# A two-layer graph network on 128 graphs: other step orders in the first two groups and the last, one statistic later in every cycle, other banks and store queues at the end

## The chip, the cores and the metric

The kernel runs on one core of one Trainium2 chip. The metric is the device time of one execution in microseconds (us); the median of several runs is compared. The engines are TensorE (PE in the profile, its weight loads PEld), VectorE (DVE), ScalarE (ACT), GpSimd (POOL) and SyncE (SP). Each works through its own queue of instructions in order.

## The reference

There are 128 graphs of 128 nodes with 512 features, all float32, and one adjacency matrix for all. Two layers follow each other; cut to what matters:

```python
# layer 0
h = relu(layernorm(x))
q, k, v = h @ Wq.T, h @ Wk.T, h @ Wv.T
rel = adj.T * (q @ k.T);  rel = rel / norm(rel, axis=2)
x = x + rel @ v
# layer 1, 8 heads of 64
h = relu(layernorm(x))
q, k, v = h @ Wq + bq, h @ Wk + bk, h @ Wv + bv
weights = softmax(q @ k.T / 8 + where(adj == 0, -1e9, 0))     # per head
x = x + weights @ v
```

## The kernel before

**Groups.** The graphs go through in 32 groups of 4 (b = 0 to 3). In a cycle three neighbouring groups are in work at once. The names in the lists of steps are: `p` the layer 1 that is being finished, `l` the layer 1 in work, `n` the layer 1 that begins, `m` the layer 0 in work, `f` the layer 0 that begins (its loads and statistics). The same object moves from `f` to `m` and from `n` to `l` to `p` (`run`, line 691, and the loop behind it).

**The order is written out by hand.** The scheduling is manual on all five engines (line 704). A step such as `l.wt0` is the method `wt(0)` of `l`; `l.Q.P1` is a step of its product Q. Each step issues instructions to several engines, and every engine executes its own in the order of the list. So a step that waits holds up everything that later steps put on the same engine. Four lists exist: FIRST (line 657, group 0), SECOND (664, group 1), ORDER (673, groups 2 to 31), LAST (684, what is left after the loop).

**Products.** A product (Q, K, V, or G, layer 0's combined query and key matrix) of a group's 512x512 block takes seven blocks of 8 matmuls, P1 to P7, in place of eight, with sums of quarters of weights and inputs formed ahead (`sumA`, `sumB`). It uses three PSUM banks x, y, z of the pool `ps_mm` (4 banks). P1 writes x and its result is kept as r1, P2 writes y and r1 is added on DVE, P5 writes z and is kept as r5, P6 adds to x and is kept as r2, P3 adds to z and r2 is added, P7 adds to x and r5 is added, P4 adds to x and is copied. P7 may only write x once r2 has been read from it, P4 only once P7's sum has been read. "Kept" is a copy on ACT, but on DVE for layer 1's V (line 246, with the bias).

**Layer 0.** `R` (line 393) multiplies, `mask_rel` (402, DVE) masks the result out of its PSUM bank, `square`, `N` and `norms` give the norms, `O` and `xO` (433, 439) the output, added to x. `O2` and `O3` read v's second half, which P4 copies on ACT.

**Layer 1.** `S` (471) makes a graph's scores for 8 heads: into one double bank `ps_s` (there is one), or, for b == 1, into the two banks of the pool `ps_o`, one half each. `mk`, or `add_mask` and `mx`, or `mkA` and `mkB` for halves, add the mask and take the maximum on DVE (483 to 488, 541 to 544); `ex`, or `exC`/`exD`, `exA`/`exB` for halves, take the exponential on ACT (495, 524, 554) and end with a DMA that sends the weights to DRAM in 32x32 blocks (`send_blocks`, line 195, on ACT's queue). `wr` fetches them back (203, SP's queue, 4 DMAs into the pool `tpool`, 2 buffers), and `wt` (508, 510) turns the blocks on DVE, so that the weights stand transposed. `A` (616) multiplies them with v, `oc` (627, ACT) copies and sends the outcome, `rdo` fetches it, and `ot` (639 to 652) turns it on DVE, scales it by 1/sum, adds x on POOL and stores to `out` on POOL's queue. The buffers of exponentials, sent inputs and outcomes are the tag "e" of the pool `npool` (3 slots). A slot is handed out in the order in which the slots were given up in the list.

In LAST the last two graphs go another way: `tw` (565, 566) transposes the weights on PE through PSUM banks of `ps_o`, ACT copies them, `An` (576) multiplies, and `fin` (585, 593, 594) scales on DVE, adds x and stores on SP's queue.

**The next input.** `hn` (312, ACT) normalizes two graphs and sends them, `rd` fetches, `T` (324, DVE) turns them. `stat` (294, 295, DVE) and `inv` (301 to 304, POOL) prepare its scale and shift.

Of the kernel before, what the change touches and what calls it, by code (L numbers as in the profile page):

```python
# [21 lines left out]
def kernel(  # L22
# [418 lines left out]
    class Layer1(Layer):  # L441
# [16 lines left out]
        def S(self, b):  # L458
            g = self.g

            if b == 1 and g < NG - 1:
                half = [ps_o.tile([P, NH, P], F32, tag="po", name=f"pso_{g}_{r}") for r in range(2)]
            else:
                pss = ps_s.tile([P, 2, NH, P], F32, tag="ps", name=f"pss_{g}_{b}")
                half = [pss[:, r] for r in range(2)]
                self.ps[b] = pss.rearrange("p r k j -> p (r k) j")
            self.half_s[b] = half
            for k in range(NH):
                for r in range(2):
                    rows = slice(r * HD, (r + 1) * HD)  # L470
                    nc.tensor.matmul(  # L471
                        half[r][:, k, :],
                        lhsT=self.qT[rows, k, ts(b, P)], rhs=self.kT[rows, k, ts(b, P)],
                        start=True, stop=True,
                    )
# [72 lines left out]
        def ex_r(self, b, r):  # L548
            g, sc, nmax = self.g, self.ps[b], self.nmax[b]
            if r == 0:  # L550
                self.total[b] = small.tile([P, H], F32, tag="total", bufs=4, name=f"total_{g}_{b}")
                self.e[b] = npool.tile([P, H, P], F32, tag="e", name=f"en_{g}_{b}")
            for i in range(r * NH, (r + 1) * NH):
                nc.scalar.activation(
                    self.e[b][:, i, :], sc[:, i, :], AF.Exp,
                    bias=nmax[:, i : i + 1], accum_out=self.total[b][:, i : i + 1],
                )
# [12 lines left out]
        def An(self, b):  # L570

            po, wT = ps_o.tile([P, D], F32, tag="po", name=f"pn1_{self.g}_{b}"), self.wT.pop(b)
            for r in range(2):
                for k in range(NH):
                    i = 2 * k + r
                    nc.tensor.matmul(
                        po[:, ts(i, HD)], lhsT=wT[:, r * NH + k, :], rhs=self.v[:, b, ts(i, HD)],
                        start=True, stop=True,
                    )
            self.po[b] = po  # L580

        def fin(self, b):
            g, xb = self.g, x_tiles.pop((self.g, b))
            o = work.tile([P, D], F32, tag="o", name=f"o_{g}_{b}")
            nc.vector.tensor_tensor(
                o.rearrange("p (k r d) -> p k r d", k=NH, r=2),
                self.po.pop(b).rearrange("p (k r d) -> p k r d", k=NH, r=2),
                self.rs.pop(b).rearrange("p (r k) -> p k r", r=2)[:, :, :, None].to_broadcast(
                    [P, NH, 2, HD]
                ),  # L590
                ALU.mult,
            )
# [37 lines left out]
        def rdo(self, i):  # L630
            self.uo[i] = fetch_blocks(self.do.pop(i), 2, f"o_{self.g}_{i}")

        def ot(self, i):
            g, u = self.g, self.uo.pop(i)
            for n in range(2):
                b = 2 * i + n
                xb = x_tiles.pop((g, b))
                o = work.tile([P, NH, TB, BK], F32, tag="o", name=f"o_{g}_{b}")
                nc.vector.transpose(
                    o.rearrange("p k t q -> p t k q"),  # L640
                    u[:, n * TB : (n + 1) * TB].rearrange("p t (k q) -> p t k q", q=BK),
                )
                heads = o.rearrange("p k t q -> p k (t q)").rearrange("p k (r d) -> p k r d", r=2)
                nc.vector.tensor_tensor(  # L644
                    heads, heads,
                    self.rs.pop(b).rearrange("p (r k) -> p k r", r=2)[:, :, :, None].to_broadcast(
                        [P, NH, 2, HD]
                    ),
                    ALU.mult,
                )  # L650
                nc.gpsimd.tensor_tensor(xb, xb, o.rearrange("p k t q -> p (k t q)"), ALU.add)  # L651
                nc.gpsimd.dma_start(out[g * G + b], xb)

# [102 lines left out]
```

## Time and profile before

| | |
|---|---|
| median of 3 runs | 2506.55 us (2505.88 to 2507.48) |
| profiled execution, whole | 2507.47 us |
| its span, first to last instruction | 2505.70 us |
| PE busy / DVE busy / ACT busy / POOL busy | 2488.6 / 1716.3 / 1024.3 / 531.5 us |
| granted TensorE clock, mean | 0.998 |
| one ordinary cycle (Q.P1 of one group to Q.P1 of the next) | 76.73 us |
| PE's last matmul ends at | 2497.43 us |

Times are microseconds from the span's start. In the views of groups and waits a line reads: line, engine, operation, output <- inputs, number, then busy time and mean, then idle time ahead. In a view of waits it reads: who waited for whom, total, times, longest. In a view of stretches it reads: the stretch, its length, the busy time of PE, PEld, DVE, ACT and POOL with the number of instructions, the granted clock (1.00 is full speed), the DMA engines' share and GB/s. Ends of matmuls are modelled, so starts are the surer times.

### The profile page before, as it was taken

To read this page: it belongs to the slowest core of one execution; us is meant where nothing else is said; L and a number is where in the kernel's file an instruction comes from. 1 tells how busy PE (TensorE), PEld (TensorE's weight loads), DVE (VectorE), ACT (ScalarE), POOL (GpSimd) and SP (SyncE) were. 2 spreads that over 40 slices of the span, in tenths; PEclk is the share of its full clock that TensorE was granted. 3 is DMA by queue.
4 is the path that set the end of the run, shared out by engine and by line. 5 is a ranking of instruction groups with operands and counts; after the bars stand their busy time and mean duration, and the time that the engine had idled before them with its cause. 6 is when DMAs were issued, how large, how long until landed. Compare 5 with 4: busy or idle time off the path is not lost.

```text
span 2505.7 us, 40908 instructions
## 1 busy us (share of the span) xinstructions
PE 2488.6 (99%) x14688; PEld 2114.5 (84%) x14688; DVE 1716.3 (68%) x2547; ACT 1024.3 (41%) x3248; POOL 531.5 (21%) x944
## 2 busy tenths in 40 slices
PE   9999999999999999999999999999999999999998
PEld 7788888888888888888888888888888888888887
DVE  6467766667766677666677666776667776667766
ACT  3334434344434444343434344443434443444433
POOL 5011212212221212122121211221221212112211
PEclk9999999999999999999999999999999999999999
DMA  6155644555544555455564455554455644455543
GB/s 207 60 169 168 189 142 156 162 177 177 161 153 153 178 164 190 139 159 169 168 185 156 155 152 179 166 184 145 151 169 169 193 147 153 155 177 177 166 137 118
DMA packets 370476, 405.72 MB, mean 162 GB/s; under 512 B 29601, under 2 KB 286753, under 8 KB 370273
## 3 DMA queue, kind: packets, MB, share of 16 engines
q1 hardware_dynamic: 279520, 168.97, 25.3%
q10 hardware_dynamic: 69856, 165.70, 17.6%
q0 software_dynamic: 20896, 68.44, 8.3%
q8 instruction: 116, 1.90, 0.3%
q14 instruction: 88, 0.71, 0.1%
HBM read 204.80 MB, written 198.18 MB: 161 GB/s over the span
## 4 chain that ended last, share of the span: by engine, by line
PE 95%; DMA 2%; DVE 1%; ACT 1%; issue 0%; SPq 0%; POOL 0%; ACTq 0%; DVEq 0%; POOLq 0%
PE pv_x L229 17%; PE pg_x L229 9%; PE pv_z L229 9%; PE pk_x L229 8%; PE pq_x L229 8%; PE pg_z L229 5%; PE pq_z L229 4%; PE po L616 4%; PE pr L393 4%; PE pk_z L229 4%; PE po L433 4%; PE pv_y L229 4%; PE pss L471 4%; PE pg_y L229 2%; PE pk_y L229 2%; PE pq_y L229 2%
## 5 line engine op out<-in xcount | busy, mean ns | idle before, releaser
L651 POOL TENSOR_TENSOR xb<-xb,o 128x512 f32<-128x512 f32 x124 | 158.0, 1274 | 1205.6 <-DVE o L644 1204.1
L229 PE MATMUL pv_x<-wc_v,h 128*128 128x256 f32 x1280 | 303.8, 384 | 0.0
L229 PEld LDWEIGHTS pv_x<-wc_v,h 128*128 128x128 f32 x1280 | 238.0, 190 | 58.6 <-issue 20.8
L229 PE MATMUL pv_z<-wc_v,s 128*128 128x256 f32 x1024 | 245.9, 383 | 0.0
L312 ACT ACTIVATE hn<-xb,shift,rstd 128x512 f32<-128x512 f32 x252 | 191.0, 807 | 127.0 <-POOL shift L304 124.8
L324 DVE STREAM_TRANSPOSE h<-u_h 128x1024 f32<-128x1024 f32 x126 | 156.1, 1239 | 107.1 <-DMA u_h<-d_h 106.9
L229 PEld LDWEIGHTS pv_z<-wc_v,s 128*128 128x128 f32 x1024 | 192.6, 190 | 28.9 <-issue 0.2
L495 ACT ACTIVATE e<-pss,nmax 128x128 f32<-128x128 f32 x512 | 179.9, 381 | 89.5 <-DVE nmax L488 75.0
L627 ACT COPY oT<-po 128x512 f32<-128x512 f32 x124 | 72.6, 586 | 274.1 <-PE po L616 274.1
L229 PE MATMUL pq_x<-h,wc_q 128*128 128x256 f32 x768 | 181.8, 380 | 0.9 <-DVE h L324 0.8
L229 PE MATMUL pv_x<-wc_v,s 128*128 128x256 f32 x768 | 181.7, 379 | 0.0
L229 PE MATMUL pk_x<-h,wc_k 128*128 128x256 f32 x768 | 181.5, 379 | 0.0
L294 DVE BATCH_NORM_STATS2 st<-xb 128x6 f32<-128x512 f32 x256 | 170.8, 667 | 8.4 <-DMA xb<-in_x_dram 8.4
L510 DVE STREAM_TRANSPOSE wT<-u_w 128x1024 f32<-128x1024 f32 x126 | 153.4, 1218 | 21.0 <-DMA u_w<-d_w 18.4
L229 PEld LDWEIGHTS pq_x<-h,wc_q 128*128 128x128 f32 x768 | 145.4, 190 | 22.1 <-PE pv_x L229 2.0
L229 PEld LDWEIGHTS pk_x<-h,wc_k 128*128 128x128 f32 x768 | 145.8, 190 | 19.9
L229 PEld LDWEIGHTS pv_x<-wc_v,s 128*128 128x128 f32 x768 | 143.3, 190 | 18.4 <-issue 0.2
L644 DVE TENSOR_TENSOR o<-o,rs 128x512 f32<-128x512 f32 x124 | 124.4, 1003 | 4.3
L229 PE MATMUL pg_z<-s,wc_a 128*128 128x256 f32 x512 | 124.1, 385 | 0.0
L301 POOL TENSOR_SCALAR rstd<-mv 128x2 f32<-128x2 f32 x128 | 28.4, 222 | 447.5 <-DVE mv L295 445.2
L616 PE MATMUL po<-wT,v 128*64 128x128 f32 x1984 | 122.0, 276 | 0.0
L229 PE MATMUL pq_z<-s,wc_q 128*128 128x256 f32 x512 | 121.6, 380 | 0.3
(157 smaller groups left out, 4834.5 us busy)
## 6 DMA issues: line engine op xcount, KB each, us to landing
d_h<-hn ACTq DMA_DIRECT2D x126, 512.0 KB, 3.6
u_h<-d_h SPq DMA_DIRECT2D x504, 128.0 KB, 3.5
d_w<-e ACTq DMA_DIRECT2D x126, 512.0 KB, 2.7
u_w<-d_w SPq DMA_DIRECT2D x504, 128.0 KB, 3.2
xb<-in_x_dram POOLq DMA_DIRECT2D x124, 256.0 KB, 3.1
d_o<-oT ACTq DMA_DIRECT2D x62, 512.0 KB, 3.0
u_o<-d_o SPq DMA_DIRECT2D x248, 128.0 KB, 2.9
out_dram<-xb POOLq DMA_DIRECT2D x124, 256.0 KB, 3.0
```

The lines of the kernel that those rows point to most:

```text
L229: nc.tensor.matmul(ps[:, m, :], lhsT=lhsT, rhs=rhs, start=first and m == 0 and k == 0, stop=k == 1, skip_group_check=True,)
L294: nc.vector.bn_stats(st, x_tiles[g, b])
L312: nc.scalar.activation(hn[:, r], x_tiles[g, b].rearrange("p (k j q) -> p j k q", j=TB, q=BK), AF.Relu, bias=self.shift[:, b : b + 1], scal ...
L324: nc.vector.transpose(half.rearrange("p k (t i) -> p t k i", i=BK), self.u.pop(i).rearrange("p t (k q) -> p t k q", q=BK),)
L393: nc.tensor.matmul(pr[:, b, :], lhsT=self.turned(k, b), rhs=self.gT[:, k, ts(b, P)], start=(k == 0), stop=(k == KD - 1),)
L433: nc.tensor.matmul(po, lhsT=self.rel[:, b, :], rhs=self.v[:, b, :], start=True, stop=True)
L471: nc.tensor.matmul(half[r][:, k, :], lhsT=self.qT[rows, k, ts(b, P)], rhs=self.kT[rows, k, ts(b, P)], start=True, stop=True,)
L495: nc.scalar.activation(e[:, :, i, :], sc[:, i, :].rearrange("p (j q) -> p j q", q=BK), AF.Exp, bias=nmax[:, i : i + 1], accum_out=self.tot ...
L510: nc.vector.transpose(self.wT[b].rearrange("p h (t i) -> p t h i", i=BK), self.uw.pop(b).rearrange("p t (h q) -> p t h q", q=BK),)
L616: nc.tensor.matmul(po[r * HD : (r + 1) * HD, k, :], lhsT=self.v[:, b, ts(2 * k + r, HD)], rhs=wT[:, r * NH + k, :], start=True, stop=True,)
L644: nc.vector.tensor_tensor(heads, heads, self.rs.pop(b).rearrange("p (r k) -> p k r", r=2)[:, :, :, None].to_broadcast([P, NH, 2, HD]), ALU ...
L651: nc.gpsimd.tensor_tensor(xb, xb, o.rearrange("p k t q -> p (k t q)"), ALU.add)
```

## The change

In FIRST, `f.G.P1` and `f.sumA` come before the last two outputs of layer 0, `n.T0` before `f.G.P7`, `n.Q.P1` before `f.G.P4`, and `w.sumk` later. In SECOND, `l.wt0` comes after `l.wr1`. In ORDER, `f.stat3 f.inv1` come after `l.V.P6`. In LAST, `p.A1 p.oc1 p.rdo1` come right after `l.S0`, graph 1 and graph 3 take their scores in halves from `ps_o`, `l.wt0` and the steps around it stand elsewhere, the last `ot` is split in two, the transposes `tw` use `ps_mm`, the last graph's `An` and `fin` are done in two halves, the sum with x of graph 2 moves from DVE to POOL, and the last stores go to SP's and ACT's queues. The last `rdo` fetches into a slot of tag "e".

```diff
-    def fetch_blocks(d, n: int, name: str):
+    def fetch_blocks(d, n: int, name: str, pool=tpool, tag="u"):
-        u = tpool.tile([P, n * TB, 8 * BK // n], F32, tag="u", name=f"u_{name}")
+        u = pool.tile([P, n * TB, 8 * BK // n], F32, tag=tag, name=f"u_{name}")
...
         def S(self, b):
-            if b == 1 and g < NG - 1:
+            if b == 1 or (b == 3 and g == NG - 1):
...
         def ex_r(self, b, r):
-            g, sc, nmax = self.g, self.ps[b], self.nmax[b]
+            g, sc, nmax = self.g, self.half_s[b][r], self.nmax[b]
...
         def tw(self, b):
-                pt = ps_o.tile([P, NH, P], F32, tag="po", name=f"pw_{g}_{b}_{r}")
+                pt = ps_mm.tile([P, NH, P], F32, tag="mm", name=f"pw_{g}_{b}_{r}")
...
         def An(self, b):
-            po, wT = ps_o.tile([P, D], F32, tag="po", name=f"pn1_{self.g}_{b}"), self.wT.pop(b)
...
+            wT, self.po[b] = self.wT.pop(b), []
+            parts = 2 if b == G - 1 else 1
+            n = NH // parts
+            for t in range(parts):
+                pool, tag = (ps_mm, "mm") if parts > 1 else (ps_o, "po")
+                po = pool.tile([P, 2 * n * HD], F32, tag=tag, name=f"pn1_{self.g}_{b}_{t}")
+                for k in range(n):
+                    for r in range(2):
+                        i = 2 * (t * n + k) + r
+                        nc.tensor.matmul(
+                            po[:, ts(2 * k + r, HD)], lhsT=wT[:, r * NH + t * n + k, :],
+                            rhs=self.v[:, b, ts(i, HD)], start=True, stop=True,
+                        )
+                self.po[b].append(po)
...
         def fin(self, b):
-            (nc.vector if b >= G - 2 else nc.gpsimd).tensor_tensor(xb, xb, o, ALU.add)
-            nc.sync.dma_start(out[g * G + b], xb)
+            n = NH // len(pos)
+            for t, po in enumerate(pos):
+                cols = slice(2 * t * n * HD, 2 * (t + 1) * n * HD)
...
+                (nc.vector if b == G - 1 else nc.gpsimd).tensor_tensor(
+                    xb[:, cols], xb[:, cols], o[:, cols], ALU.add
+                )
+                (nc.scalar if b == G - 2 else nc.sync).dma_start(out[g * G + b][:, cols], xb[:, cols])
...
         def rdo(self, i):
-            self.uo[i] = fetch_blocks(self.do.pop(i), 2, f"o_{self.g}_{i}")
+            last = i == 1 and self.g == NG - 2
+            where = (npool, "e") if last else (tpool, "u")
+            self.uo[i] = fetch_blocks(self.do.pop(i), 2, f"o_{self.g}_{i}", *where)
         def ot(self, i):
...
+            for n in range(2):
+                self.ot_n(i, n)
+        def otA(self, i):
+            self.ot_n(i, 0)
+        def otB(self, i):
+            self.ot_n(i, 1)
+        def ot_n(self, i, n):
...
+            late = i == 1 and g == NG - 2
+            queue = (nc.sync, nc.scalar)[n] if late else nc.gpsimd
+            queue.dma_start(out[g * G + b], xb)
...
     FIRST = """
...
-        n.inv0 m.V.P4 n.hn0 n.rd0 f.T1 m.O2 m.xO2 m.O3 m.xO3 n.stat2 n.stat3 n.inv1 f.sumA f.start f.G.P1
-        f.G.P2 f.sumB w.sumk f.G.P5 n.hn1 n.rd1 f.G.P6 f.G.P3 f.G.P7 n.T0 f.G.P4 n.T1 n.start
+        n.inv0 m.V.P4 n.hn0 n.rd0 f.T1 f.start f.G.P1 f.sumA m.O2 m.xO2 m.O3 m.xO3 n.stat2 n.stat3 n.inv1
+        f.G.P2 f.sumB f.G.P5 n.hn1 n.rd1 f.G.P6 f.G.P3 n.T0 n.start f.G.P7 n.Q.P1 w.sumk f.G.P4 n.T1
     SECOND = """
-        l.Q.P1 l.sumA l.Q.P2 l.sumB l.K.P1 l.K.P2 l.Q.P5 l.Q.P6 f.load0 f.load1 l.Q.P3 l.K.P5 l.K.P6 l.Q.P7
+        l.sumA l.Q.P2 l.sumB l.K.P1 l.K.P2 l.Q.P5 l.Q.P6 f.load0 f.load1 l.Q.P3 l.K.P5 l.K.P6 l.Q.P7
...
-        m.V.P2 m.V.P5 l.wt0 m.R m.mask_rel m.square f.stat2 f.stat3 f.inv1 m.V.P6 l.S1 m.N l.S2 l.mkA1 m.norms l.exC1
-        l.mkB1 l.exD1 l.wr1 m.V.P3 l.add_mask2 m.V.P7 l.mx2 l.exC2 m.O0 m.xO0 m.O1 m.xO1 n.stat0 n.stat1 n.inv0
+        m.V.P2 m.V.P5 m.R m.mask_rel m.square f.stat2 f.stat3 f.inv1 m.V.P6 l.S1 m.N l.S2 l.mkA1 m.norms l.exC1
+        l.mkB1 l.exD1 l.wr1 l.wt0 m.V.P3 l.add_mask2 m.V.P7 l.mx2 l.exC2 m.O0 m.xO0 m.O1 m.xO1 n.stat0 n.stat1 n.inv0
...
     ORDER = """
...
         l.wr2 n.hn0 n.rd0 l.start_v f.stat2 l.V.P1 m.O2 m.xO2 m.O3 m.xO3 n.stat2 n.stat3 n.inv1 l.V.P2 l.V.P5 l.wt1
-        f.stat3 f.inv1 n.hn1 l.V.P6 l.wt2
+        n.hn1 l.V.P6 f.stat3 f.inv1 l.wt2
         n.rd1 l.V.P3 l.V.P7 n.T0 l.S3 l.A0 l.mk3 l.oc0 l.V.P4 l.ex3 n.T1 n.start
     LAST = """
         l.Q.P1 p.rdo0 l.sumA l.Q.P2 p.wr3 l.sumB l.K.P1 l.K.P2 p.ot0 l.Q.P5 l.Q.P6 l.Q.P3 p.wt3 l.K.P5 l.K.P6 l.K.P3
-        l.Q.P7 l.S0 l.mk0 l.K.P7 l.ex0 l.wr0 l.Q.P4 l.K.P4 l.S1 l.mk1 p.A1 p.oc1 p.rdo1 l.start_v l.V.P1
-        l.ex1 l.V.P2 l.V.P5 l.S2 l.mkA2 l.mkB2 l.V.P6 l.exA2 l.exB2 l.wt0 l.wr1 l.V.P3 l.V.P7 l.S3 l.mkA3 l.mkB3
-        l.tw2 l.wt1 l.exA3 l.exB3 l.V.P4 l.An0 l.fin0 l.An1 l.fin1 p.ot1 l.tw3 l.An2 l.fin2 l.An3 l.fin3
+        l.Q.P7 l.S0 p.A1 l.mk0 p.oc1 p.rdo1 l.K.P7 l.ex0 l.wr0 l.Q.P4 l.K.P4 l.S1 l.mkA1 l.exC1 l.start_v l.V.P1
+        l.mkB1 l.exD1 l.wr1 l.V.P2 l.wt0 l.V.P5 l.S2 l.S3 l.mkA2 l.exA2 l.mkB2 l.exB2 l.V.P6 l.mkA3 l.exA3 l.V.P3
+        l.V.P7 l.tw2 l.wt1 l.mkB3 l.exB3 l.V.P4 l.An0 l.fin0 l.An1 p.otA1 l.fin1 l.tw3 p.otB1 l.An2 l.fin2
+        l.An3 l.fin3
```

More of the change, by code (lines that the diff above doesn't have):

```diff
@@ L554, in ex_r @@
                 nc.scalar.activation(
-                    self.e[b][:, i, :], sc[:, i, :], AF.Exp,
+                    self.e[b][:, i, :], sc[:, i - r * NH, :], AF.Exp,
                     bias=nmax[:, i : i + 1], accum_out=self.total[b][:, i : i + 1],
@@ L570, in An @@
         def An(self, b):
-            po, wT = ps_o.tile([P, D], F32, tag="po", name=f"pn1_{self.g}_{b}"), self.wT.pop(b)
[L573 to L580, printed above, removed]
+            wT, self.po[b] = self.wT.pop(b), []
@@ L582, in fin @@
         def fin(self, b):
-            g, xb = self.g, x_tiles.pop((self.g, b))
+            g, xb, rs, pos = self.g, x_tiles.pop((self.g, b)), self.rs.pop(b), self.po.pop(b)
             o = work.tile([P, D], F32, tag="o", name=f"o_{g}_{b}")
[L585 to L592, printed above, removed]
@@ L593, in fin @@
-            (nc.vector if b >= G - 2 else nc.gpsimd).tensor_tensor(xb, xb, o, ALU.add)
-            nc.sync.dma_start(out[g * G + b], xb)
+            n = NH // len(pos)
+            for t, po in enumerate(pos):
+                cols = slice(2 * t * n * HD, 2 * (t + 1) * n * HD)
+                nc.vector.tensor_tensor(
+                    o[:, cols].rearrange("p (k r d) -> p k r d", k=n, r=2),
+                    po.rearrange("p (k r d) -> p k r d", k=n, r=2),
+                    rs.rearrange("p (r k) -> p k r", r=2)[:, t * n : (t + 1) * n, :, None].to_broadcast(
+                        [P, n, 2, HD]
+                    ),
+                    ALU.mult,
+                )
+                (nc.vector if b == G - 1 else nc.gpsimd).tensor_tensor(
+                    xb[:, cols], xb[:, cols], o[:, cols], ALU.add
+                )
+                (nc.scalar if b == G - 2 else nc.sync).dma_start(out[g * G + b][:, cols], xb[:, cols])
@@ L630, in rdo @@
         def rdo(self, i):
-            self.uo[i] = fetch_blocks(self.do.pop(i), 2, f"o_{self.g}_{i}")
+            last = i == 1 and self.g == NG - 2
+            where = (npool, "e") if last else (tpool, "u")
+            self.uo[i] = fetch_blocks(self.do.pop(i), 2, f"o_{self.g}_{i}", *where)
         def ot(self, i):
-            g, u = self.g, self.uo.pop(i)
             for n in range(2):
[L636 to L652, printed above, removed]
@@ new lines, in ot @@
+                self.ot_n(i, n)
[4 more added lines that the diff above has]
+        def ot_n(self, i, n):
+            g, u = self.g, self.uo[i]
+            b = 2 * i + n
+            xb = x_tiles.pop((g, b))
+            o = work.tile([P, NH, TB, BK], F32, tag="o", name=f"o_{g}_{b}")
+            nc.vector.transpose(
+                o.rearrange("p k t q -> p t k q"),
+                u[:, n * TB : (n + 1) * TB].rearrange("p t (k q) -> p t k q", q=BK),
+            )
+            heads = o.rearrange("p k t q -> p k (t q)").rearrange("p k (r d) -> p k r d", r=2)
+            nc.vector.tensor_tensor(
+                heads, heads,
+                self.rs.pop(b).rearrange("p (r k) -> p k r", r=2)[:, :, :, None].to_broadcast(
+                    [P, NH, 2, HD]
+                ),
+                ALU.mult,
+            )
+            nc.gpsimd.tensor_tensor(xb, xb, o.rearrange("p k t q -> p (k t q)"), ALU.add)
+            late = i == 1 and g == NG - 2
+            queue = (nc.sync, nc.scalar)[n] if late else nc.gpsimd
+            queue.dma_start(out[g * G + b], xb)
```

## The prediction

> **What bounds the kernel now.** I read the page first: PE is busy 99% of the span and the chain that ended last is 95% PE.
>
> ```profile
> PE 2488.6 (99%) x14688; PEld 2114.5 (84%) x14688; DVE 1716.3 (68%) x2547; ACT 1024.3 (41%) x3248; POOL 531.5 (21%) x944
> ...
> PE 95%; DMA 2%; DVE 1%; ACT 1%; issue 0%; SPq 0%; POOL 0%; ACTq 0%; DVEq 0%; POOLq 0%
> ```
>
> The edits remove no matmul, so only waits of PE, and what stands after its last matmul, can be gained. Next, the waits of PE:
>
> ```profile
> PE pso L471 <- DVE rel L402: 3.7, 1, 3.7
> ...
> PE pg_x L229 <- DVE gT L253: 0.8, 1, 0.8
> PE pq_x L229 <- DVE h L324: 0.8, 2, 0.5
> PE po L433 <- ACT v L237: 0.7, 1, 0.7
> PE pw L565 <- DVE o L585: 0.5, 1, 0.5
> ```
>
> Small sums, and the first is worth more than it says. Stretches of the timeline (us; PE, PEld, DVE, ACT, POOL busy; granted clock), cut around it:
>
> ```profile
> 104.80:107.90 3.10, 0.00 (x0) 0.00 (x0) 1.25 (x2) 0.00 (x0) 0.00 (x0) 1.00 0.16 47
> 107.90:114.75 6.85, 6.22 (x42) 5.12 (x43) 5.00 (x10) 4.07 (x18) 2.37 (x5) 0.50 0.00 0
> ```
>
> PE stands 3.7 us, then runs at half clock for 6.8 us. Another set of stretches holds the same steps (R of layer 0 up to the next Q.P1) in group 1, in an ordinary cycle, and in the last cycle, which has no next group and so no stat3:
>
> ```profile
> 98.90:138.57 39.67, 35.43 (x218) 28.84 (x216) 23.85 (x41) 12.37 (x42) 5.08 (x13) 0.91 0.43 134
> 183.59:215.70 32.11, 32.11 (x218) 26.36 (x216) 25.63 (x45) 12.48 (x42) 8.86 (x21) 1.00 0.51 165
> 2411.48:2443.41 31.93, 31.93 (x218) 26.45 (x217) 22.84 (x35) 12.47 (x42) 4.94 (x11) 1.00 0.48 152
> ```
>
> 218 matmuls each: 31.93 is their price without a wait. The timeline of PE gives a block of 8 matmuls 1.73 us everywhere.
>
> **What the Trainium skill says.** "TensorE: Matmul & The Clock Gate", part 1, What's actually happening: after an idle window of about 3.4 us the array drops to half rate and comes back after a busy window. The trace agrees: 3.7 us idle, 6.8 us at 0.50. "SBUF — State Buffer", Who interferes with whom: VectorE with two SBUF inputs and a GpSimd op reading SBUF block each other. The trace agrees: xb+o on DVE took 1.46 us beside POOL's add (at 2497.70) and 0.69 alone (2499.79). "DMA: Bandwidth & Descriptors", Latency and other measured facts: a store from GpSimd starts later than one from SP or ACT. Here POOL's last took 2.66 us (2498.90 to 2501.56), SP's last 2.10 (2500.51 to 2502.61). No run here shows ACT's queue storing the output.
>
> **SECOND (group 1).** DVE reaches l.wt0 at 99.2 and stands until u_w lands at 106.53; mask_rel is queued behind it, S1 needs mask_rel's bank, and PE waits. With wt0 after exD1, mask_rel runs at 102.7–103.4 (pr ends 102.48), before S1 at 104.30; no wait, no half clock. Where does wt0 go? mkA1 and mkB1 end at about 108.45 (S1 ends 105.4; two halves of 1.4 us and norms' 0.3), the data is there since 106.53, wt0 takes 0.2+1.25 to 109.85, and behind it P3's sum ends at 110.45. O0 needs that sum and is due at 110.39: 0.1 us. Then add_mask2 (1.2) and P7's sum end at 112.2, V.P4 due at 112.2: 0.05. mx2 is later, so exC2, exD2, d_w2, u_w2 and wt2 come some 0.6 us later against PE than in an ordinary cycle, where P3's sum ends 0.98 us ahead of A0: 0 to 0.2. T0 costs 0 to 0.9 (below). So 39.67 − 31.93 = 7.74, less 0.25: **7.5** (6.5 to 7.8). The cycle after it took 77.13 against 76.73 (Q.P1 to Q.P1), as cycles after a late T0 do; that goes too: **0.4**.
>
> **FIRST (group 0).** Now V.P4 ends at 52.47, O2 waits for its ACT copy until 53.31 (0.83); G.P7 ends at 65.49, G.P4 waits for DVE's sum until 66.43 (1.05 with its start-up). After: G.P1 covers the first, Q.P1 the second. The price is on the queue of hn1. O2/O3 come 1.73 later less the 0.83, sumA (1.37) stands ahead on DVE, so stat3 ends at 59.0 instead of 57.69; POOL's inv1 took 3.1 us beside DVE's two-input ops, 1.6 where alone (94.48–96.06): shift at 60.7 to 61.5. hn1 (1.52), its DMA issue and the copy of r2 are queued on ACT, so r2 is free at 63.3 to 64.1, where G.P7 is due at 62.93. G.P7, then Q.P1 (T0 done in time), G.P4, then Q.P2 at r2 + 5.4: 68.8 to 69.6, against 69.99 now. Q.P2's bank is the slot that G.P2 gave up, since the program hands out the slot freed first, so it does not wait for G.P4's copy. sumk (2.75 us) moves behind P7's sum: K.P5 needs it 8 us later; T1 ends at about 71.5, Q.P5 is due at 74.7. **0.7** (−0.2 to 1.2).
>
> **ORDER: one statistic later.** The timeline of DVE: wt1 ends 207.53, stat3 and its aggregate 207.46–208.32, then P6's r2 at 208.24–208.90; PE's P6 ended at 207.15, P7 waits for r2 until 208.95 (P3 1.81 and P7 1.92 us, where the last cycle has 1.73 and 1.82). After: r2 at 207.5–208.2, P7 at once: 0.18 a cycle. What stat3 then delays is wt2, by at most 0.87 us; it stood waiting for its DMA until 209.13 anyway, and if the data were early A0's 0.98 us of room covers it. inv1 moves 0.7 us later on POOL, idle for 15 us after it. 29 cycles (g=2 to 30); in three (Q.P1 at 369, 1905 and 2136) Q.P1 follows T0 within 0.15 us, T0 hangs on a late u_h, and the 0.18 is given back. 26 × 0.18 = **4.7** (3.8 to 5.2).
>
> **LAST.** PE now loses 0.35 (S1 for ex0's bank), 0.17, 0.56 (S3 for exB2's bank) and 0.63 (tw3 for ot1 and fin1 on DVE). After: S1 and S3 use the two po banks, A1 moves ahead, pw gets mm banks. Worked forward from S0 at 2462.49: A1 2463.58, K.P7 2465.5, K.P4 to 2470.8, S1, V.P1 2472.05, V.P2, V.P5, S2 2477.3, S3, P6 2479.6, P3 2481.33, P7 due at 2483.06. On ACT oc1 (now ahead of ex0) ends at 2466.2 and its issue takes 0.4, so ex0 starts 0.4 later and d_w0 goes at 2469.6. On SP rdo1 waits for d_o (lands about 2470) and ends 2472.6, just before d_w0 lands at 2472.9; wr0 as before, u_w0 at about 2478.1. wt0 holds DVE until 2479.35; behind it r5, mkA2, mkB2 and r2, at 2483.3: P7 loses 0.3 (to 1.0 if u_w0 is 0.7 later). exB2 ends 2484.25 ahead of tw2 (2485.1); u_w1 lands about 2486.3, wt1, mkB3, exB3 to 2490.5 ahead of tw3 (2491.55). PE ends at 2496.2, not 2497.43. Buffers: uo1 now keeps one of the three "e" slots to the tail, so en2 takes e0's (its send landed at 2472.9, exA2 comes at 2481.4) and en3 e1's (about 2481 against 2484.7): no wait. The stores of otB1 and fin2 are queued on ACT, which has nothing after tw3's copies; those of fin0, otA1, fin1 and fin3 on SP, idle by then. POOL takes five adds of 1.27 from 2490.7 on, fin2's (now POOL's) the last, to about 2498; fin3's second half of xb+o waits for it, 2498.6; its store goes out about 1.85 us earlier than now (2500.51) and lands near 2500.9.
>
> The end is not that store alone. SP was through at 2503.00, but the instruction records show POOL's closing drain from 2498.87 to 2504.92, behind its own store, and only then the last 0.78 us to 2505.70. Afterwards POOL's last store is p.ot0's, 40 us earlier. The cost of a drain without one isn't shown at the end (at the start it took 0.17 us). Bounds: nothing, then SP sets the end, 2500.9 + 0.39 + 0.78 = 2502.1, gain 3.6; or the same 5.5 us after POOL's last instruction, 2498 + 5.5 + 0.78 = 2504.3, gain 1.4. I take the first: the work drained is that of the store. **3.6** (1.0 to 4.3).
>
> **Sum.** 7.5 + 0.4 + 0.7 + 4.7 + 3.6 = 16.9. Span 2505.70 − 16.9 = 2488.8; that execution took 2507.47, so 1.77 around it: 2490.6; its time was 0.92 over the median, so **2489.6**.
>
> **Rivals.** (1) POOL's drain stays 5.5 us without a store: 2489.6 + 2.2 = 2491.8. For it: a drain may be fixed; against: 0.17 at the start. (2) The cycle is held by DMA, not by r2: T0 has 0.15 to 1.4 us of room before Q.P1 depending on how fast u_h lands (5.5 us, 7.1 in SECOND), and each T0 is issued from work before P6; if most cycles give the 0.18 back and SECOND's T0 waits its 0.9: 2489.6 + 4.7 = 2494.3. Against: 24 of the 29 cycles show 0.65 us of room or more. (3) Slower: a DVE wait takes the place of the one removed, at LAST's wt0, which moves from 2482.4 up to where its data lands, with r5, mkA2, mkB2 and r2 behind it and P7 behind r2. Each us of u_w0 beyond 2477.8 is a us of PE; from 3.1 us on the clock halves too, 3.4 more. Not slower becomes slower when it eats 16.9, so with u_w0 13.5 us late; the longest fetch seen on this path is 7.1 where I count 5.6. That it does nothing at all would need SECOND's 7.7 us to stay: mask_rel would have to wait on something other than wt0, and DVE shows no other.
>
> **Chances.** Forecast as worked out 0.62; rival 1 0.20; rival 2 0.11; rival 3 or another new stall of over 12 us 0.07 (0.04 of it within 0.2%, 0.03 slower). 0.2% is 5 us, about what a measurement of this kernel can tell (its three runs lie within 1.6). Faster 0.93, same 0.04, slower 0.03. Best ends together give 2487.3, less run scatter 2486; worst ends 2495.2, which also holds rivals 1 and 2: 2486 to 2495.5.
>
> **What would show it.** Right: clock 1.00 throughout group 1 and no PE wait on rel; R to Q.P1 about 32.2 us there; cycles of 76.55 us; G.P7, not G.P4, waiting in FIRST; POOL's drain under 1 us and SP closing. Wrong: u_h or u_w0 landing over 2 us later than here, an idle PE of over 3 us anywhere with clock 0.50 behind it, or cycles still at 76.73.

## The result, and the profile after

The changed kernel takes 2497.28 us (median of 6 runs, 2496.85 to 2499.45), the kernel before in the same session 2506.42 (6 runs, 2505.50 to 2507.48): a ratio of 0.9967, 95% interval 0.9956 to 0.9977. It is faster by 9.1 us, 0.33%. The forecast was 16.9 us and 2489.6, with a range up to 2495.5: the direction was right, the size was not, and the time lies outside the range.

The profiled executions differ by more than the medians: span 2505.70 before, 2495.44 after, 10.26 us, mainly because the profiled execution of before lies 1.05 us over its median. The terms below are taken from these two traces and add up to 10.26.

The page of the changed kernel, parts 1 and 4, the lines that answer to those shown of before:

```profile
PE 2480.9 (99%) x14688; PEld 2116.5 (85%) x14688; DVE 1716.0 (69%) x2550; ACT 1024.7 (41%) x3248; POOL 530.8 (21%) x943
...
PE 93%; DVE 2%; DMA 2%; ACT 1%; issue 0%; SPq 0%; POOL 0%; ACTq 0%; DVEq 0%; POOLq 0%
```

PE's share of the chain is 93% where it was 95%: more of the chain now runs over other engines (the page does not say where). The waits of PE in the changed kernel (who waited for whom, total us, times, longest):

```profile
PE pq_x L229 <- DVE h L324: 2.2, 4, 1.1
PE idle L123 <- POOL ident masks.py:199: 1.4, 1, 1.4
PE pv_x L229 <- DVE pv_r L246: 1.3, 1, 1.3
PE pn L581 <- DVE o L593: 0.9, 1, 0.9
PE pg_x L229 <- ACT pg_r L237: 0.8, 1, 0.8
```

The 3.7 us on `rel` are gone, as forecast. But three lines are larger or new. Q.P1 (`pq_x`) waits for T0 (`h`) 2.2 us in place of 0.8. `pv_x <- pv_r` (V.P7 on r2) and `pn <- o` (An1 on fin0) stand in the last group, where none of this was expected. The stretches from R of layer 0 to the next Q.P1 in group 1, in the first ordinary cycle and in the last cycle (length, busy PE, PEld, DVE, ACT, POOL, granted clock, DMA share, GB/s):

```profile
98.99:132.28 33.29, 32.16 (x217) 26.18 (x216) 23.62 (x41) 12.40 (x42) 5.07 (x13) 1.00 0.54 166
177.31:209.24 31.93, 31.93 (x218) 26.47 (x217) 25.52 (x45) 12.48 (x42) 8.84 (x21) 1.00 0.50 164
2401.25:2433.17 31.92, 31.92 (x217) 26.47 (x216) 22.89 (x35) 12.48 (x42) 4.93 (x11) 1.00 0.47 151
```

Group 1 runs at full clock (1.00, before 0.91 over the stretch) in 33.29 us in place of 39.67. The ordinary stretch has come down from 32.11 to 31.93, the price without a wait. Group 1 still lies 1.36 us above it.

| Term (us gained) | forecast | from the two traces |
|---|---|---|
| up to FIRST (loads and weights) | 0 | −0.71 |
| FIRST | 0.7 | 0.63 |
| SECOND, R to Q.P1 | 7.5 | 6.38 |
| SECOND's late start no longer felt in the next cycle | 0.4 | 0 |
| ORDER | 4.7 | 3.95 |
| LAST, from its Q.P1 to the end | 3.6 | 0.02 |
| sum | 16.9 | 10.27 (span: 10.26) |

The first row is a difference of the two executions at the start of the program, in a part that is the same in both: the last eight matmuls of the weight work (`pa`, line 127) start at 17.10 us against 16.39. The largest miss is LAST: its Q.P1 to the end of the program took 62.29 us before and 62.27 after.

### The profile page after: what moved, and what is told of

Its sections match the earlier page's. It is cut to its first block, busy times and chain, and to the rows that moved or that the text cites. A ratio compares the mean times of both kernels' runs of the same rounds, so it can differ in the third digit from the quotient of the medians.

```text
span 2495.4 us, 40875 instructions
## 1 busy us (share of the span) xinstructions
PE 2480.9 (99%) x14688; PEld 2116.5 (85%) x14688; DVE 1716.0 (69%) x2550; ACT 1024.7 (41%) x3248; POOL 530.8 (21%) x943
## 4 chain that ended last, share of the span: by engine, by line
PE 93%; DVE 2%; DMA 2%; ACT 1%; issue 0%; SPq 0%; POOL 0%; ACTq 0%; DVEq 0%; POOLq 0%
PE pv_x L229 16%; PE pg_x L229 9%; PE pv_z L229 8%; PE pq_x L229 8%; PE pk_x L229 8%; PE pr L393 5%; PE pg_z L229 5%; PE pq_z L229 4%; PE pk_z L229 4%; PE po L626 4%; PE pv_y L229 4%; PE po L433 4%; PE pss L471 4%; PE pg_y L229 2%; PE pq_y L229 2%; PE pk_y L229 2%
```

## The experiments

Four take the change apart, five change something in the last group, one moves another suspect. The kernel before ran beside each: 2506.01 us (38 runs) for the four that take the change apart, 2505.28 (10 runs) for pool_early, pool_late, mk_together and phase128, 2506.11 (9 runs) for an1_bank and the three together. Ratios carry 95% intervals. "Below before" is the difference of the two medians.

### The change without its last group

```diff
 the kernel before, with three lists of the changed one:
-    FIRST, SECOND, ORDER as before
+    FIRST, SECOND, ORDER as changed
     LAST and all methods as before
```

> The kernel before with the new lists of the first two groups and of the cycle, and the old last group. Theory from the two traces: the new last group nets nothing (62.29 us from its first Q.P1 to the end before, 62.27 after), so this takes what the whole change takes, 2497.3 us, within 1. Rival: the last group gave its forecast 3.6 us and the shortfall lies in the first three parts: 2500.9.

Measured: 2495.36 us (2493.81 to 2496.51), ratio 0.9958 (0.9945 to 0.9972), 10.7 below before; more than the 9.1 of the whole change, and more than the theory's 1 us from it. The rival, in which the new last group brings 3.6, would have put this run at 2500.9, and falls. The new last group brings nothing. Whether it costs 1.5 us, as the two medians say, is not shown: in this trace Q.P1 waited 0.6 us in all where the changed kernel's waited 2.2, which has nothing to do with the last group, and from the last Q.P1 to the end it took 62.30 us (62.27 in the changed kernel).

### SECOND alone

```diff
-        m.V.P2 m.V.P5 l.wt0 m.R m.mask_rel ...
-        l.mkB1 l.exD1 l.wr1 m.V.P3 ...
+        m.V.P2 m.V.P5 m.R m.mask_rel ...
+        l.mkB1 l.exD1 l.wr1 l.wt0 m.V.P3 ...
```

> The kernel before with l.wt0 moved behind l.wr1 in group 1 and nothing else. Theory: the wait for rel and the half clock go (7.7 us), u_h's slow fetch (7.1 to 7.5 us) takes back 1.3 of it as a wait of Q.P1: 39.67 becomes about 33.3, 6.4 to 6.6 us in all, 2499.9. As forecast: 7.9 us, 2498.5. Rival: the half clock comes back at the later wait: gain under 4, above 2502.

Measured: 2499.81 us (10 runs), ratio 0.9976 (0.9967 to 0.9985), 6.2 below before, as the trace of the whole change had it. In this profiled execution Q.P1 came at 130.82 without any wait for T0: R (98.82) to Q.P1 took 32.00 us, 7.67 less than before, and the next cycle 76.73, the ordinary value of the old ORDER. So the 1.1 us of the changed kernel's trace isn't the price of moving wt0; it comes and goes (see the shifted program below). This execution gained what had been forecast for SECOND; the median of the ten runs did not.

### ORDER alone

```diff
-        f.stat3 f.inv1 n.hn1 l.V.P6 l.wt2
+        n.hn1 l.V.P6 f.stat3 f.inv1 l.wt2
```

> The kernel before with f.stat3 and f.inv1 one step later in every cycle and nothing else. Theory: 29 cycles of 0.18 us, 5.2 us, of which cycles whose Q.P1 hangs on u_h give back 1 to 1.5: 3.8, 2502.6. As forecast: 4.7, 2501.7. Rival: the cycle is held by the DMA throughout: 0 to 1, above 2505.4.

Measured: 2501.71 us (21 runs), ratio 0.9983 (0.9977 to 0.999), 4.3 below before, between the theory's 3.8 and the forecast's 4.7, which the medians can't tell apart. The rival, 0 to 1, falls. The timelines (start, us, engine, line, operation) decide how a cycle went. Before, PE and DVE:

```profile
207.15 1.89 PE L229 MATMUL pv_z<-wc_v,s 128*128 128x256 f32 x8
207.46 0.65 DVE L294 BATCH_NORM_STATS2 st<-xb 128x6 f32<-128x512 f32 x1
208.24 0.66 DVE L246 TENSOR_TENSOR pv_r<-pv_x,bv_sb 128x512 f32<-128x512 f32 x1
208.95 2.00 PE L229 MATMUL pv_x<-wc_v,h 128*128 128x256 f32 x8
```

In the changed kernel:

```profile
200.87 1.89 PE L229 MATMUL pv_z<-wc_v,s 128*128 128x256 f32 x8
201.18 0.65 DVE L246 TENSOR_TENSOR pv_r<-pv_x,bv_sb 128x512 f32<-128x512 f32 x1
201.75 0.67 DVE L294 BATCH_NORM_STATS2 st<-xb 128x6 f32<-128x512 f32 x1
202.59 1.89 PE L229 MATMUL pv_x<-wc_v,h 128*128 128x256 f32 x8
```

P6's copy r2 (`pv_r`, 201.18) now runs ahead of the statistic (201.75). P3 starts at 200.87 and P7 at 202.59, 1.72 later, where it was 1.80; from P7 to S3's scores it is 1.82 (204.41 less 202.59) where it was 1.93 (210.88 less 208.95). An undisturbed cycle took 76.55 us in place of 76.73, in line with the 0.18 of the forecast.

### LAST alone

```diff
 the changed kernel, with three lists of the one before:
-    FIRST, SECOND, ORDER as changed
+    FIRST, SECOND, ORDER as before
     LAST and all methods as changed
```

> The kernel before with the new last group and its new store queues and nothing else. Theory: two waits of PE come (V.P7 1.37, An1 0.9) for the four that go (1.71), and POOL's drain stays 5.3 us behind POOL's last instruction, which comes no earlier: 2506.4, within 0.7. As forecast: 3.6 us, 2502.8. Rival: PE's later end counts: 2507.1.

Measured: 2506.79 us (13 runs), ratio 1.0003 (0.9995 to 1.0011): 0.8 above before, and the interval includes 1, no difference at all. The forecast's 2502.8 falls; the theory's 2506.4 and the rival's 2507.1 can't be told apart. The parts run alone sum to −6.2 − 4.3 + 0.8 = −9.7 (FIRST was not run alone; with the −0.6 that its trace says it is −10.3), against −9.1 for the whole.

### The last group: who closes the program

The timeline of POOL at the end of the changed kernel, the last three of its five sums:

```profile
2484.97 1.27 POOL L601 TENSOR_TENSOR xb<-xb,o 128x512 f32<-128x512 f32 x1
2486.87 1.26 POOL L672 TENSOR_TENSOR xb<-xb,o 128x512 f32<-128x512 f32 x1 [0.63 <-DVE o L665]
2488.09 1.26 POOL L601 TENSOR_TENSOR xb<-xb,o 128x512 f32<-128x512 f32 x1
```

POOL ends its last sum at 2489.36. SP is through with the last store at 2492.37. But the instruction records give POOL's closing drain up to 2494.68, 5.32 us after the sum, and only then the last 0.76 us to 2495.44. There is no store on POOL's queue at that point. In the kernel before, POOL's last line was a store's issue, and its drain ended at 2504.92:

```profile
2498.90 0.56 POOL L652 DMA_DIRECT2D out_dram<-xb  x1 [0.30 <-POOL xb L651]
```

Two kernels move POOL's last instruction, in opposite directions.

```diff
 pool_early: the sums of otB1 and fin2 go to DVE
-                (nc.vector if b == G - 1 else nc.gpsimd).tensor_tensor(
+                (nc.vector if b >= G - 2 else nc.gpsimd).tensor_tensor(
...
-            nc.gpsimd.tensor_tensor(xb, xb, o.rearrange("p k t q -> p (k t q)"), ALU.add)
+            (nc.vector if late and n else nc.gpsimd).tensor_tensor(xb, xb, o.rearrange(...), ALU.add)
```

> The changed kernel with the sums with x of otB1 and fin2 on DVE in place of POOL; POOL's last instruction is fin1's sum. Theory: the end stands some 5.3 us plus 0.8 behind POOL's last instruction, whatever that is, so it moves until SP sets it: POOL's last at about 2486.3 of 2495.4, SP through at about 2492.4, then 0.8: span 2493.2, 2.2 us less, 2495.1. Theory of the forecast (the drain belongs to POOL's stores): no change, 2497.3. Rival: DVE, with two sums more, ends later: 2498.

Measured: 2493.68 us (2493.19 to 2494.49), ratio 0.9953 (0.994 to 0.9965), 11.6 below before where the changed kernel is 9.1 below: 2.5 more, where 2.2 was expected. POOL's last sum ended at 2484.21 and its drain at 2489.53, 5.32 later again. SP, through at 2490.67, now sets the end of 2491.41. From the last Q.P1 to the end it is 60.37 us in place of 62.27, 1.9 less, although in this execution the clock stood at 0.50 from 2480.55 to 2483.97 and PE's last matmul came 56.37 us after Q.P1 (54.68 in the changed kernel).

```diff
 pool_late: one small instruction on POOL behind fin3, no store
+            if b == G - 1:
+                nc.gpsimd.tensor_scalar(o[:, D - 2 : D], o[:, D - 2 : D], 1.0, None, ALU.mult)
```

> The changed kernel with one more POOL instruction of 128x2 elements behind fin3's last sum, no store. Theory: POOL's last instruction goes from 2489.4 to about 2490.8 and the end with it: 1.4 us more, 2498.7, with a drain of 5.3 us again. Theory of the forecast: an instruction without a store has no long drain: no change, 2497.3.

Measured: 2498.01 us (2496.88 to 2501.22), ratio 0.9971 (0.996 to 0.9983). The median lies between the two expectations and settles nothing. The instruction records do: POOL's 128x2 operation ended at 2493.33 and the drain at 2498.65, 5.32 later, with SP through at 2494.89, 3.8 us earlier. So three traces show the same 5.32 us behind an instruction that is no store, and the five other traces with the new last group show it too. In the traces that end with a store on POOL's queue (the kernel before, and the change without its last group) it is 5.47 us after the store's issue: 2499.45 to 2504.92, and 2485.79 to 2491.26. The drain's end follows POOL's last instruction at a nearly constant distance. What it waits for in that time, no run here shows.

This trace shows something else as well. PE's stretches around its last waits (length, busy times, granted clock):

```profile
2471.79:2481.51 9.72, 7.35 (x49) 6.60 (x48) 8.74 (x16) 5.49 (x26) 0.44 (x1) 1.00 0.08 19
2481.51:2491.90 10.39, 10.39 (x51) 10.33 (x50) 5.53 (x8) 1.17 (x2) 5.89 (x5) 0.50 0.29 109
```

PE stands 1.5 and 0.9 us in the first stretch, and from 2481.51 on the clock is at 0.50: An2 and An3 take longer (6.93 us for their 32 matmuls, 3.68 in the changed kernel's trace). The Trainium skill, "TensorE: Matmul & The Clock Gate", part 1, What's actually happening, speaks of an idle window of about 3.4 us. In this trace a stretch of that length ahead of the fall (2478.10 to 2481.51) holds 0.85 us of idle time, An1's wait, and the rest is An0's and An1's matmuls. So here the half clock came without such a window. It is not the only trace in which it did; they stand together under what stays open.

### The last group: what PE waits for

The timelines of DVE, PE and ACT in the changed kernel, with what ended the idle time in brackets:

```profile
2469.71 0.69 DVE L544 TENSOR_REDUCE nmax<-pss 128x4 f32<-128x512 f32 x1
...
2472.02 0.70 DVE L541 TENSOR_TENSOR pss<-pss,mask 128x512 f32<-128x512 f32 x1 [1.62 <-ACT en L554]
2472.76 0.69 DVE L544 TENSOR_REDUCE nmax<-pss 128x4 f32<-128x512 f32 x1
2473.36 0.68 DVE L246 TENSOR_TENSOR pv_r<-pv_x,bv_sb 128x512 f32<-128x512 f32 x1
...
2474.10 1.99 PE L229 MATMUL pv_x<-wc_v,h 128*128 128x256 f32 x8 [1.30 <-DVE pv_r L246]
...
2480.71 0.69 DVE L593 TENSOR_TENSOR o<-pn,rs 128x512 f32<-128x512 f32 x1 [0.68 <-PE pn L581]
...
2481.46 0.88 PE L581 MATMUL pn<-v,wT 128*128 128x64 f32 x6 [0.85 <-DVE o L593]
```

mkA2 ends at 2470.40, and mkB2 (2472.02) then waits 1.62 us for exA2's last exponential (`en`, ACT). LAST lists them as mkA2 exA2 mkB2 exB2. The kernel before listed mkB2 ahead of exA2, and there it followed mkA2 at once, with the exponentials behind both (the chain of the kernel before):

```profile
2478.87 0.71 DVE pss L541
...
2480.33 0.71 DVE pss L541
...
2481.84 2.91 ACT en L554 x16
```

The two halves of graph 2 stand in the two banks of one tile, and in the new order mkB2 would write its half while exA2 reads the other: the built program makes mkB2 wait for exA2's last exponential. Where the halves are tiles of their own it does not: in group 1 of the changed kernel's trace graph 1's mkB1 starts at 107.15, beside exC1's exponentials (from 107.08 to 108.59). r2 of V.P6 (`pv_r`, 2473.36) is queued behind mkB2 on DVE, and V.P7 behind r2. The second wait: An1 waits for fin0's multiply, which reads An0's bank of `ps_o`, so it seems to have been given the same bank. Two kernels take away one of these each.

```diff
 mk_together
-        ... l.S3 l.mkA2 l.exA2 l.mkB2 l.exB2 l.V.P6 ...
+        ... l.S3 l.mkA2 l.mkB2 l.exA2 l.exB2 l.V.P6 ...
```

> The changed kernel with mkA2 mkB2 exA2 exB2 in the last group in place of mkA2 exA2 mkB2 exB2. Theory: mkB2 waits 1.6 us on DVE for exA2, since both halves lie in one tile; then r2 and V.P7 behind it are late. Together: no such wait, V.P7 1.3 us earlier, all that follows too: 2496.0. Rival: DVE is simply full there: no change in V.P7's wait, 2497.3.

Measured: 2494.50 us (2493.04 to 2498.46), ratio 0.9957 (0.9943 to 0.9971), 10.8 below before. The theory had 2496.0 and the rival 2497.3; the five runs scatter over 5.4 us, and the ratio's interval overlaps with that of the changed kernel, so the time alone does not settle it. The timeline of DVE in this kernel:

```profile
2469.68 0.69 DVE L541 TENSOR_TENSOR pss<-pss,mask 128x512 f32<-128x512 f32 x1
2470.40 0.69 DVE L544 TENSOR_REDUCE nmax<-pss 128x4 f32<-128x512 f32 x1
2471.12 0.70 DVE L541 TENSOR_TENSOR pss<-pss,mask 128x512 f32<-128x512 f32 x1
2471.86 0.69 DVE L544 TENSOR_REDUCE nmax<-pss 128x4 f32<-128x512 f32 x1
2472.47 0.68 DVE L246 TENSOR_TENSOR pv_r<-pv_x,bv_sb 128x512 f32<-128x512 f32 x1
```

mkB2 follows mkA2 without a wait, and V.P7's wait is 0.50 in place of 1.30. (What is left here: wt0's data landed at 2467.74, 0.7 us later than in the changed kernel's trace.) That settles the wait, and the rival falls. The time that it is worth is not shown by this trace: in this execution the clock fell to 0.50 from 2481.71 to 2485.12, and the last group took 62.05 us, 0.2 less than in the changed kernel.

```diff
 an1_bank
-                pool, tag = (ps_mm, "mm") if parts > 1 else (ps_o, "po")
+                pool, tag = (ps_mm, "mm") if b % 2 else (ps_o, "po")
```

> The changed kernel, with An1 writing a bank of ps_mm in place of the one bank of ps_o that An0 also has; nothing else. Theory (the end hangs on DVE and POOL, not on PE): PE no longer waits 0.85 us for fin0's multiply and its last matmul ends 0.8 us earlier after Q.P1 (53.9 in place of 54.69), but fin1's multiply stays behind otA's 1.62 us on DVE, so POOL's last sum and its closing drain stay where they are: 62.2 us from Q.P1 to the end, time 0 to 0.3 us below the changed kernel's 2497.3 (8.7 to 9.4 below before) where the granted clock stays full. And with one short wait less before it, the half clock in the last group is rarer: in at most one run of the five the mean granted clock is 0.998 or less. Rival (PE is what the tail waits for): the whole 0.85 comes off, about 2496.4, 10 below before.

Measured: 2495.89 us (2495.03 to 2497.16), ratio 0.9962 (0.9949 to 0.9974). The median is 10.2 below before, and the ratio, times 2506.11, says 9.5: the first is the rival's, the second near the theory's, so the trace has to tell. PE's last matmul ends 53.67 us after Q.P1 in place of 54.68, but POOL's last sum ends 56.21 after it (56.18 in the changed kernel), and the end comes 62.30 after it (62.27). The timeline of DVE shows why:

```profile
2479.93 0.69 DVE L593 TENSOR_TENSOR o<-pn,rs 128x512 f32<-128x512 f32 x1 [0.69 <-PE pn L581]
2480.54 0.70 DVE L660 STREAM_TRANSPOSE o<-u_o 128x512 f32<-128x512 f32 x1
2481.28 1.60 DVE L665 TENSOR_TENSOR o<-o,rs 128x512 f32<-128x512 f32 x1
2482.81 0.68 DVE L593 TENSOR_TENSOR o<-pn,rs 128x512 f32<-128x512 f32 x1
```

fin1's multiply (2482.81) stands behind otA's on DVE, whether An1 is early or not. An1's wait is gone, so it was one for An0's bank; but it was hidden in the tail, and the theory holds. One run of the five had a mean granted clock of 0.998, the others 0.999, as had been expected; but that run (2495.22 us) is the second shortest, so the mean does not mark a run that lost time.

### The three together

```diff
 all_mended: the edits of pool_early, mk_together and an1_bank in one kernel
```

> The changed kernel with three edits in the last group together: mkB2 ahead of exA2, An1 in a bank of ps_mm, the sums of otB1 and fin2 on DVE. Theory: PE's waits in the last group come to 0.6 us at most in place of 2.15, the clock stays at 1.00 to PE's end in every run (mean granted clock 0.999), POOL's last instruction ends 2484 or earlier, its drain 5.3 us later is over before SP's last store, and SP sets the end: 12 to 13.5 us below before, about 2492.5 to 2493.5 if before is at 2505.5. Rival (DVE's queue alone holds the tail, PE's waits were hidden): no better than the two sums moved alone, which gave 11.6 below before, and the runs scatter as those of the changed kernel do.

Measured: 2492.07 us (2491.45 to 2493.01), ratio 0.9947 (0.9933 to 0.996): 14.0 below before, more than pool_early's 11.6; the times of the two kernels' runs do not overlap, though the ratios' intervals do. In pool_early's profiled execution a stretch at half clock is part of the difference. PE's only wait in the last group is now

```profile
PE pv_x L229 <- DVE pv_r L246: 0.2, 1, 0.2
```

and in this trace the clock is at 1.00 up to 2486.16, past PE's last matmul (2484.54); the mean granted clock is 0.999 in all five runs. From Q.P1, PE's last matmul ends after 52.56 us (54.68 in the changed kernel), POOL's last sum after 52.01, and the program after 58.89 in place of 62.27. This is 3.4 us better than the kernel before (62.29), near the 3.6 of the forecast for LAST. The median lies 0.4 us below the theory's bounds and the gain 0.5 above. This version beats both kernels. Together the edits are shown to give what LAST lacked; of the single edits only pool_early's runs lie clear of those of the changed kernel.

### What makes Q.P1 late

In the changed kernel's trace Q.P1 waited for T0 at 132, 363, 747 and 2127 us, and the profile's queues list a fetcher that no step of the program issues:

```profile
q8 instruction: 116, 1.90, 0.3%
```

116 packets of 16 KB. From one packet to the next PE executes 256 instructions on average (that would be 64 bytes each, an estimate from these two figures), so this looks like the stream of PE's own instructions. The late T0s are those whose u_h fetch (the four DMAs of `rd` that bring T0's data, usually 5.4 to 5.9 us) took 6.7 to 7.5 us, and in each a q8 packet started 3.1 to 4.2 us behind the fetch's issue. If the packet's place in PE's stream is the cause, then more PE instructions at the start must move the late cycles elsewhere; if some place of the kernel is the cause, they stay.

```diff
 phase128: 32 small products (128 PE instructions) ahead of the first; their results are not used
+        for _ in range(32):
+            nc.tensor.matmul(
+                idle[0:BK, :], lhsT=ones, rhs=ident, start=True, stop=True, skip_group_check=True
+            )
```

> The changed kernel with 32 more small matmuls (128 instructions of PE's stream) in front of the first product; their result isn't used. Theory: a Q.P1 is late where a 16 KB fetch of PE's own instructions (one in 256 instructions) falls 3 to 4.3 us behind the issue of u_h's fetch. With 128 instructions more the late ones move: the five at 132, 363, 747, 1742 and 2127 us (fetch of u_h 6.7 to 7.5 us) come down to about 5.5 us, and those at 286, 670, 1053, 1436, 1819 and 2204 (5.4 to 5.6 us) go up to 6.5 or more. Rival: the lateness belongs to the places, that is to other transfers beside u_h: the same five stay late. Time: 1 to 3 us more for the head, in both.

Measured: 2504.16 us, a single profiled run that says little of time (the first Q.P1 came 6.4 us later than in the changed kernel, where 1 to 3 had been expected). From the traces, the fetch ahead of Q.P1, cycle by cycle (us; "behind" is when a q8 packet started after the fetch's issue):

```
cycle of group   changed kernel             128 instructions more
                 Q.P1     fetch  behind     Q.P1     fetch  behind
1                132.28   7.51   3.8        137.40   5.66   none
3                285.79   5.46   none       290.71   6.58   4.0
4                363.06   7.17   4.1        367.66   5.99   none
8                669.66   5.52   none       674.47   7.05   4.1
9                746.59   6.82   4.0        751.42   5.67   none
13              1053.19   5.47   none      1058.05   6.45   3.6
18              1436.09   5.46   none      1441.38   6.71   3.5
22              1742.42   6.66   4.2       1747.98   5.51   none
23              1819.37   5.47   none      1825.28   7.12   4.0
27              2126.57   6.84   3.1       2131.88   5.64   none
28              2203.52   5.49   none      2209.12   7.13   4.1
```

All five moved away, six others came. The late starts belong to the place of PE's instruction fetch, not to those cycles. A packet that starts 4.4 us or more behind the issue does no harm in these two traces (for instance 5.42 us for the fetch of the cycle at 209.24, with a packet 5.2 behind). All twelve traces say the same of the fetches ahead of the Q.P1 of groups 1 to 31: the 227 without a packet took at most 6.1 us; of the 58 with a packet 2.6 to 4.2 behind all but one took 6.2 to 7.6; with a packet within the first 1.6 us or later than 4.2, all but one (7.0, in SECOND alone) took at most 6.3. Group 1 shows the same in the traces of all kernels that have the new SECOND: with a packet 3.6 to 3.9 us behind, Q.P1 waited 1.1 to 1.2 us (the changed kernel, pool_early, an1_bank, all_mended), with one 2.6 behind 0.3 (mk_together), with none in the fetch not at all (the change without its last group, SECOND alone, pool_late). Why the packet falls into this fetch in some executions and 3.7 us ahead of it in others isn't settled.

## Why the prediction was off, step by step

- **SECOND's mechanism, right.** No wait on `rel`, clock 1.00, mask_rel at 102.76 to 103.45, wt0 ending at 109.76 where 109.85 was worked out, O0 0.07 us longer where 0.1 was counted. Where T0 is punctual, as in the trace of SECOND alone, 7.67 us were gained.
- **"T0 costs 0 to 0.9", mis-sized.** u_h took 7.51 us, and Q.P1 waited 1.1. The term of 7.5 became 6.38. The late start has its echo: the next cycle takes 0.4 longer (76.95 in place of 76.55), so the **0.4** wasn't gained either. Together 1.5 us.
- **FIRST, right.** G.P7 waits for r2 (0.8 us, `pg_x <- pg_r`), not G.P4, and 0.63 was gained for 0.7.
- **ORDER: 0.18 a cycle right, the number given back mis-sized.** All 29 cycles show it: 5.2. Given back were 1.27 (excess over the undisturbed cycle: 4.39 us after, 3.12 before), where the forecast took three cycles of 0.18, 0.5. A T0 that is late by a given time costs Q.P1 0.18 more in a shorter cycle, and a Q.P1 that is made late costs 0.4 more in the next. Nor were there only three such cycles before: at 753.53 and 1751.38, too, T0 ended only 0.22 and 0.28 us ahead of Q.P1. The late cycles had been put down to a slow u_h as such, without asking what made it slow. 3.95 for 4.7. The excess differs from trace to trace: 2.4 to 5.2 us in the eight traces with the new ORDER (phase128 apart), 2.5 to 3.1 in the three with the old one; the means differ by 1.3 too.
- **LAST: three steps failed.** (1) "r5, mkA2, mkB2 and r2, at 2483.3": the forecast let mkB2 follow mkA2 at once, though the new list puts exA2 between them; the halves of the double bank are one tile, and mkB2 waited 1.62 us for exA2. With r2 queued behind it, V.P7 waited 1.3 us where 0.3 was forecast. (2) PE ended 54.68 us after Q.P1, 0.66 later than before instead of 1.23 earlier: besides V.P7's wait, An1 waited for fin0's multiply (0.85), a wait that the prediction put at nothing without naming An1's bank; by the rule of its FIRST, the slot freed first, An1 would have had the bank of S3's other half. (3) "I take the first: the work drained is that of the store": POOL's drain costs 5.32 us with no store. The end of the kernel was POOL's 2489.36 + 5.32 + 0.76 = 2495.44. Step 3 alone is 2.3 us (SP was through at 2492.37). The rest of the 3.6 is put down to steps 1 and 2: with all three mended the term came to 3.4. That is not shown for each alone: in the trace without An1's wait the end did not move, and in the one without mkB2's wait it moved by 0.2 with the clock lost.
- **The stores, right.** ACT's queue, which no run had shown with a store of the output, landed its first in 2.07 us (2488.17 to 2490.24), close to SP's 2.10 before.
- **What had been feared at LAST's wt0 didn't come**: its data landed 33.88 us after Q.P1, where 34.69 had been counted, and DVE waited 0.76 us for it.
- **Two sums are slightly off**: the best and worst ends of the terms add up to gains of 18.9 and 11.5, so to 2487.6 and 2495.0, where the prediction has 2487.3 and 2495.2. The time lies outside either way.

Of the rivals the first (drain without a store) is what happened, alone worth 2.2. The second (late T0s) happened in part: 1.5 in SECOND and 0.75 in ORDER. They were treated as alternatives, and both came, with more that none of the rivals had: mkB2's wait and An1's. (The third rival had looked for a late V.P7 behind r2, but from wt0's data.) The range took one or the other: both in full come to 2489.6 + 2.2 + 4.7 = 2496.5, above its upper end of 2495.5.

What stays open is the clock in the last group. The eight traces with the new last group (us from the span's start; the half clock while PE still had matmuls to do):

```
trace            V.P7 waits   An1 waits   clock 0.50
changed kernel   1.30         0.85        no
LAST alone       1.21         0.85        no
pool_early       1.34         0.85        2480.55 to 2483.97
pool_late        1.51         0.85        2481.51 to PE's end
mk_together      0.50         0.85        2481.71 to 2485.12
phase128         1.67         0.85        2489.40 to 2492.82
an1_bank         1.35         none        no
all_mended       0.25         none        no
```

In each of the four that lost it, the 3.41 us before the fall hold An1's whole wait and no other idle time of PE, and V.P7's wait was over at least 8.2 us before. So the loss goes with An1's wait and not with V.P7's. But two traces have the same wait and kept the clock, so what decides it is not known. Nor is the share of the changed kernel's runs that lose it: two of its six have a mean granted clock of 0.998 or less and are its longest (2499.01 and 2499.45; the others are 2496.85 to 2497.34), but pool_early's and mk_together's traced executions lost it for 3.4 us with a mean of 0.999.

## What to carry to other kernels

Look when each engine's closing drain ends, and give the last instructions of the engine with the slowest drain to another one: taking POOL's stores away was not enough, taking its last two sums away was. When a step is split into halves, see whether the halves are separate for the program's waits or share a tile, before counting on one running beside the other. And when a transfer is now and then slow, find out what it collides with before booking it as scatter, since a shorter cycle turns the same delay into more lost time.

## What was not expected of the hardware

- POOL's closing drain ends 5.32 us after POOL's last instruction, be it a 128x512 sum (changed kernel, pool_early) or a 128x2 operation (pool_late), and 5.47 after a store's issue. In the changed kernel's trace ACT's drain ends 0.19 us after its last store's issue and DVE's 0.05 after its last sum. POOL's "0.17 at the start" was no guide to it.
- PE's instruction stream costs data transfers: packets of 16 KB, one for each 256 PE instructions (116 in the whole execution), made a 512 KB fetch take 6.5 to 7.5 us in place of about 5.5 if they started 3.1 to 4.2 us behind its issue (changed kernel, phase128).
- The granted clock fell to 0.50 in four traces with PE idle for only 0.85 us of the 3.41 us before the fall, between matmuls with 64 output columns.
